# Eight relu(x - mean) tiles of layer 0 on VectorE instead of GpSimd, in a four-layer graph attention kernel

## The chip, the core and the metric

The kernel runs on one core of a Trainium2 chip. A core has five engines that work side by side, each with a queue of its own that is worked off in order: TensorE (PE in the profile, its weight loads PEld), VectorE (DVE), ScalarE (ACT), GpSimd (POOL) and SyncE (SP), which issues most of the transfers. Engines wait for each other through semaphores. The metric is the device time of one execution in microseconds; the time before is the median of three runs, 1781.22 us (1780.12 to 1788.01).

## The reference: what is computed

A graph of 4096 nodes with 256 features each goes through four layers of attention over one dense adjacency matrix of 4096 x 4096 integers, of which few entries are set. Every layer normalises the features, takes the positive part, and adds the layer's attention output to its input:

```python
h = jnp.maximum(_layernorm(x, axis=-1), 0.0)
x = x + _L0_gnn_ref(h, adj, ...)        # layers 1 to 3 likewise

# layer 0
h = node_features @ W.T + b_W
e = (h @ a1)[:, None] + (h @ a2)[None, :] + b_a[0]
e = jnp.where(e > 0, e, 0.2 * e)
scores = jnp.where(adjacency_matrix > 0, e, NEG_INF)
attention = jax.nn.softmax(scores, axis=1)
h_prime = attention @ h
```

Layer 1 has the same form with an ELU behind it, layer 2 has four heads of 64 features, layer 3 a positive and a negative softmax. The change touches only the first line of layer 0, for some of the nodes.

## The kernel before, in words

The 4096 nodes are 32 tiles of 128 nodes (NT = 32, P = 128); a block is 512 nodes, so four tiles (IB = 512, IT = 4). The node features x stay in SBUF as one tile of 128 x 32 x 256.

**Making the nodes of a layer.** `node_rows` (line 683) works on two tiles at a time. VectorE takes mean and variance (L693, L694); ScalarE makes 1/sqrt(variance + eps) through a logarithm and an exponential (L697, L698), which three small VectorE operations refine (L709 to L711). L702 makes z = max(x - mean, 0); the scale 1/std is positive and is applied only later. In layer 0 two GpSimd additions (L706) then add the layer's bias to x in place, since x is also the residual. TensorE transposes z in two halves (L716) into PSUM, ScalarE copies the result to SBUF as hT (L718), and `project` multiplies hT with the weights (L748) and lets ScalarE write the scaled rows g with their two exponentials (L759 to L783). z has four buffers (`bufs=4`), so z of a pair of tiles needs the buffers of the pair two before it, which are free once those have been transposed. The transposes, the projections and all small matmuls share two PSUM buffers (`s_mm`, `bufs=2`).

**Weights of layer 0.** `make_weights` (line 564) multiplies weights by attention vectors on TensorE (L622, L640); VectorE scales the results into columns of the weights (L634), sums a bias (L643, L644); TensorE spreads the bias row over all partitions (L647) and ScalarE copies it out (L649). L706 and the g of layer 0 need that copy.

**Attention of layer 0.** The first four blocks of target nodes (2048 targets) are treated as dense. For every block all 32 source tiles are gone through: VectorE makes the unnormalised weights s_p of 128 sources x 512 targets (L1033), and four times TensorE adds p.T @ g into an accumulator (L1071). On the way the adjacency is read in chunks of 1 MB, two transfers of 512 KB each (`s_raw`, L1306, four buffers). VectorE turns a chunk into a byte mask (L1325), which SyncE writes to DRAM for the later layers (L1327). The chunks of the other four blocks are read at the side, one every three steps, so that lists of the sources that matter to each tile can be built (lines 819 to 912: prefix sums, one-hot matrices L875, small matmuls L900, and the list itself L910). The last 16 tiles of targets, and most of the later layers, use such lists: GpSimd gathers the rows by indirect transfers (L929, L1231).

**What sets the order.** `run` (line 1194) goes through a plan of steps with leads of 0, 2, 3 and 6 steps for fetching, starting, weighing and multiplying, and takes a few pieces of work of other kinds after each step, `node_rows` among them, from queues. GpSimd's instructions stay in that program order (`tc.manual_schedule(engines={mybir.EngineType.Pool})`, line 1496). For the other four engines the framework that builds the program decides the order in each queue, from its own estimates of durations and from what each instruction depends on. When an instruction changes engine, the order of others in all these queues can change with it.

Of the kernel before, what the change touches and what calls it, by code (L numbers as in the profile page):

```python
# [13 lines left out]
ALU = mybir.AluOpType  # L14
# [9 lines left out]
IT = IB // P  # L24
# [455 lines left out]
def list_layers(ctx: ExitStack, tc: tile.TileContext, a: dict, out: bass.AP, flag):  # L480

    nc = tc.nc
# [31 lines left out]
    x = keep.tile([P, NT, D], F32, name="x")  # L514
# [17 lines left out]
    def feature_rows(l, jt):  # L532
        return table_rows(table[l], jt)[:, :, FRONT[l] : FRONT[l] + GW[l]]
# [13 lines left out]
    def weights(l, pool, prep, q):  # L547


        L = layers[l] = Layer()  # L550
        L.l = l
        L.H, L.part = LH[l], PART[l]

        ncols = D + 3 * L.H + (D if l == 3 else 0)
        L.w = pool.tile([P, 2, ncols], F32, name=f"s_w{l}", tag=f"s_w{l}")
        L.s = small.tile([P, NT, L.H], F32, name=f"s_s{l}", tag=f"s_s{l % 2}", bufs=1)
        L.ready = [False] * NT
        L.bias = None
        L.table = table[l]
        L.made = False  # L560
        L.making = make_weights(L, pool, prep, q)
        return L
# [120 lines left out]
    def node_rows(L, T0):  # L683


        u = f"{L.l}_{T0}"
        tiles = (T0, T0 + 1)
        while any(stored[T] < L.l - 1 for T in tiles) or not L.made:
            yield
        mv = small.tile([P, 2, 2], F32, name=f"s_mv_{u}", tag="mv")  # L690
        for k, T in enumerate(tiles):
            st6 = small.tile([P, 6], F32, name=f"s_st6_{u}_{k}", tag="st6")
            nc.vector.bn_stats(st6, x[:, T, :])  # L693
            nc.vector.bn_aggr(mv[:, k, :], st6)  # L694
            yield
        r = small.tile([P, 3, 2], F32, name=f"s_r_{u}", tag="r")
        nc.scalar.activation(r[:, 0], mv[:, :, 1], AF.Ln, bias=eps)  # L697
        nc.scalar.activation(r[:, 0], r[:, 0], AF.Exp, scale=-0.5)  # L698
        zs = []
        for k, T in enumerate(tiles):  # L700
            z = rows.tile([P, D], F32, name=f"s_z_{u}_{k}", tag="z", bufs=4)
            (nc.gpsimd if L.l == 0 else nc.vector).tensor_scalar(z, x[:, T, :], mv[:, k, 0:1], 0.0, op0=ALU.subtract, op1=ALU.max)  # L702
            zs.append(z)
        if L.bias is not None:
            for T in tiles:
                nc.gpsimd.tensor_add(x[:, T, :], x[:, T, :], L.bias[:, 0:D])  # L706
        yield 1.5

        nc.vector.scalar_tensor_tensor(r[:, 1], mv[:, :, 1], EPS, r[:, 0], op0=ALU.add, op1=ALU.mult)  # L709
        nc.vector.scalar_tensor_tensor(r[:, 1], r[:, 1], -0.5, r[:, 0], op0=ALU.mult, op1=ALU.mult)  # L710
        nc.vector.scalar_tensor_tensor(r[:, 2], r[:, 1], 1.5, r[:, 0], op0=ALU.add, op1=ALU.mult)  # L711
        hTs = []
        for k, T in enumerate(tiles):
            tp = ps_mm.tile([P, 2, P], F32, name=f"s_tp_{u}_{k}", tag="mm")
            for c in range(2):
                nc.tensor.transpose(tp[:, c, :], zs[k][:, c * P : (c + 1) * P], ident)  # L716
            hT = rows.tile([P, 2, P], F32, name=f"s_hT_{u}_{k}", tag="hT")
            nc.scalar.copy(hT, tp)  # L718
            hTs.append(hT)
            yield  # L720
        yield 1.5
        for k, T in enumerate(tiles):
            g = L.rows(T)
            yield from project(L, T, g, hTs[k], r[:, 2, k : k + 1])
            L.ready[T] = True
            if L.l == 0 and T % CH == CH - 1:
                nc.sync.dma_start(feature_rows(L.l, T), L.g[:, T - CH + 1 : T + 1, :])
            elif L.l > 0:
                nc.sync.dma_start(feature_rows(L.l, T)[:, T % CH, :], g)
# [251 lines left out]
    class Unit:  # L981
# [124 lines left out]
        def end(u):  # L1106
            l = u.L.l
            for it in range(u.nt):
                T = u.T0 + it
                if l == 0:  # L1110
                    end0(T, u.accs[it])
                else:
                    work = end2(u, it, T) if l == 2 else (end1 if l == 1 else end3)(T, u.accs[it])
                    push(posts, work, (4.0, 2.5, 0.0)[l - 1])
                if l < 3 and T % 2:
                    push(posts, node_rows(layers[l + 1], T - 1))
            if u.on_end:
                u.on_end()
# [129 lines left out]
    with ExitStack() as phase:  # L1248
# [8 lines left out]
        def load_x(b):  # L1257

            nc.sync.dma_start(
                x[:, b * IT : (b + 1) * IT, :],  # L1260
                a["x"][b * IB : (b + 1) * IB, :].rearrange("(c p) d -> p c d", p=P),
            )
            for T in (b * IT, b * IT + 2):
                push(posts, node_rows(L0, T))
# [135 lines left out]
    for l in (2, 3):  # L1400
        L = weights(l, late, late, nc.sync)
# [11 lines left out]
    for l in (1, 2, 3):  # L1413
        L = layers[l]
# [131 lines left out]
```

## Time and profile before

| what | us |
|---|---|
| median of three runs | 1781.22 |
| profiled execution | 1697.57 |
| its span | 1695.8 |
| TensorE busy in the span | 1619.6 (96%) |
| VectorE busy | 1321.9 (78%) |
| GpSimd busy | 959.8 (57%) |
| ScalarE busy | 632.6 (37%) |
| first attention matmul (L1071) starts | 30.48 |
| the 32 z of layer 0 on GpSimd | 9.96 to 92 |

The page counts one execution under the profiler. A group line names the source line, the engine, the operation, what is written and read, and how often; a duration follows. In a timeline the first number is the start in microseconds from the start of the span, the second the length, and a bracket tells how long the engine had been idle and what ended that. A line of the waits names who waited for whom, the sum, the number of times and the longest. A window's row gives the busy time of each engine in that stretch. Matmuls are pipelined and their ends are modelled, so a busy TensorE need not be one at its peak. The profiled execution is 84 us shorter than the median of the runs without a profile.

### The profile page before, as it was taken

The numbers are of one execution on the slowest core, as the hardware profiler recorded it, in microseconds if no ns is written. First come the engines' busy times: TensorE is split into PE (matmuls) and PEld (weight loads), VectorE is DVE, ScalarE is ACT, GpSimd is POOL, SyncE is SP. The second block draws the span as 40 slices with busy tenths as digits, with TensorE's granted clock in tenths as the row PEclk, the third lists the DMA queues.
The fourth block names the chain that finished last, engine by engine and source line by source line (L and its number), as shares of the span: only waits on it lengthen the run. The fifth ranks groups of instructions, "written<-read, shape, count | busy, mean of one in ns | idle before, by whom it ended". The sixth has DMA issues, their size and how long they took to land.

```text
span 1695.8 us, 29208 instructions
## 1 busy us (share of the span) xinstructions
PE 1619.6 (96%) x9268; PEld 1366.4 (81%) x9268; DVE 1321.9 (78%) x3908; ACT 632.6 (37%) x1915; POOL 959.8 (57%) x930
## 2 busy tenths in 40 slices
PE   6999999899989999879999999999999999999997
PEld 4887778788868887766787787899988888888886
DVE  6888999888845786558898988988884777777765
ACT  5631010120211232333667766899991111111111
POOL 9836766757635766651555444445652655555463
PEclk9999999999989999989999999999999999999998
DMA  8899879954364545452333333333434666666554
GB/s 270 281 326 291 277 231 273 309 155 124 76 170 129 151 131 165 138 149 67 92 97 96 89 86 99 86 100 95 132 106 125 204 187 180 178 184 173 171 169 118
DMA packets 152237, 274.70 MB, mean 162 GB/s; under 512 B 21423, under 2 KB 75340, under 8 KB 152076
## 3 DMA queue, kind: packets, MB, share of 16 engines
q0 software_dynamic: 45584, 130.39, 28.7%
q1 hardware_dynamic: 105656, 141.83, 26.0%
q8 instruction: 77, 1.26, 0.3%
q14 instruction: 84, 0.69, 0.1%
q10 hardware_dynamic: 836, 0.53, 0.1%
HBM read 231.76 MB, written 40.90 MB: 161 GB/s over the span
## 4 chain that ended last, share of the span: by engine, by line
PE 52%; DMA 2%; DVE 1%; ACT 1%; issue 0%; POOL 0%; ACTq 0%; DVEq 0%; POOLq 0%
PE s_acc L1071 24%; PE s_accm L1096 22%; PE s_pj L748 3%; DMA s_gg<-table,idx 2%; PE s_sT L967 1%; PE s_tp L716 1%; PE s_oT L1158 0%; ACT s_p L1019 0%; DVE s_p L1033 0%; ACT mlist L1056 0%; DMA out<-s_out 0%; DVE s_p L1042 0%; POOL s_gg L1231 0%; DVE s_y L1187 0%; DVE s_out L1138 0%
## 5 line engine op out<-in xcount | busy, mean ns | idle before, releaser
L1231 POOL DMA_INDIRECT s_gg<-table,idx x715 | 751.7, 1051 | 643.8 <-PE s_acc L1071 219.4
L1033 DVE SCALAR_TENSOR_TENSOR s_p<-s_grow,s_gg,mlist 128x128 f32<-128x128 f32 x994 | 316.3, 349 | 103.1 <-PE s_acc L1071 55.3
L1071 PE MATMUL s_acc<-s_gg,s_p 128*128 128x257 f32 x1430 | 348.1, 387 | 6.3 <-DVE s_p L1033 6.3
L1071 PEld LDWEIGHTS s_acc<-s_gg,s_p 128*128 128x128 f32 x1430 | 268.0, 192 | 47.9 <-DVE s_p L1033 11.5
L1071 PE MATMUL s_acc<-g,s_p 128*128 128x257 f32 x1152 | 283.4, 387 | 13.2 <-DVE s_p L1033 9.1
L1071 PEld LDWEIGHTS s_acc<-g,s_p 128*128 128x128 f32 x1152 | 214.0, 192 | 46.9 <-DVE s_p L1033 14.7
L1033 DVE SCALAR_TENSOR_TENSOR s_p<-s_grow,pre,mpre 128x128 f32<-128x128 f32 (+1 forms) x576 | 191.1, 371 | 39.3 <-PE s_acc L1071 31.9
L1096 PE MATMUL s_accm<-s_p,s_gg 128*65 128x128 f32 x1744 | 204.0, 273 | 0.0
L1071 PE MATMUL s_acc<-s_gs,s_p 128*128 128x257 f32 x896 | 203.7, 380 | 0.0
L1033 DVE SCALAR_TENSOR_TENSOR s_p<-s_grow,s_gs,s_ms 128x512 f32<-128x512 f32 x224 | 162.6, 752 | 48.0 <-PE s_acc L1071 23.1
L1096 PEld LDWEIGHTS s_accm<-s_p,s_gg 128*65 128x65 f32 x1744 | 193.1, 138 | 2.5
L1019 ACT ACTIVATE s_p<-s_grow,s_minus,s_gg 128x128 f32<-128x128 f32 x436 | 186.6, 486 | 13.4 <-PE s_accm L1096 7.9
L1071 PEld LDWEIGHTS s_acc<-s_gs,s_p 128*128 128x128 f32 x896 | 169.4, 190 | 25.1 <-DVE s_p L1033 1.1
L1071 PE MATMUL s_acc<-pre,s_p 128*128 128x257 f32 x768 | 181.6, 381 | 0.0
L973 ACT ACTIVATE s_grow<-s_sT 128x256 f32<-128x256 f32 (+2 forms) x136 | 46.7, 367 | 346.9 <-PE s_sT L967 310.8
L748 PE MATMUL s_pj<-s_w,s_hT 128*128 128x259 f32 (+3 forms) x640 | 165.3, 399 | 8.4 <-ACT s_hT L718 4.4
L1071 PEld LDWEIGHTS s_acc<-pre,s_p 128*128 128x128 f32 x768 | 143.5, 191 | 20.9 <-PE s_acc L1071 0.3
L929 POOL DMA_INDIRECT mlist<-mask_t,idx x105 | 123.9, 1180 | 61.8 <-issue 29.1
L748 PEld LDWEIGHTS s_pj<-s_w,s_hT 128*128 128x128 f32 x640 | 122.2, 198 | 33.7 <-ACT s_hT L718 8.4
L1096 PE MATMUL s_accm<-s_p,pre 128*65 128x128 f32 (+1 forms) x928 | 119.6, 284 | 0.0
L1096 PEld LDWEIGHTS s_accm<-s_p,pre 128*65 128x65 f32 x928 | 103.6, 138 | 16.6 <-issue 14.0
L1019 ACT ACTIVATE s_p<-s_grow,s_minus,pre 128x128 f32<-128x128 f32 x224 | 96.4, 487 | 19.1 <-issue 11.6
(126 smaller groups left out, 1741.0 us busy)
## 6 DMA issues: line engine op xcount, KB each, us to landing
s_raw<-in_adjT SPq DMA_DIRECT2D x128, 512.0 KB
s_gs<-table SPq DMA_DIRECT2D x28, 516.0 KB
s_gg<-table,idx POOLq DMA_INDIRECT x715, 3.6
mask_t<-s_m SPq DMA_DIRECT2D x35, 256.0 KB
table<-s_g SPq DMA_DIRECT2D x28, 258.0 KB
s_ms<-mask_t SPq DMA_DIRECT2D x28, 256.0 KB
table<-s_m SPq DMA_DIRECT2D x21, 256.0 KB
table<-g SPq DMA_DIRECT2D x8, 516.0 KB
```

Of the source, the lines that this page charges most:

```text
L716: nc.tensor.transpose(tp[:, c, :], zs[k][:, c * P : (c + 1) * P], ident)
L748: nc.tensor.matmul(ps, lhsT=hT[:, c, :], rhs=L.w[:, c, k * (D + 6) : k * (D + 6) + cols], start=(c == 0), stop=(c == 1),)
L929: nc.gpsimd.indirect_dma_start(out=mlist[:, OFFS[T] + k, :], out_offset=None, in_=mask_t[T // IT], in_offset=bass.IndirectOffsetOnAxis(ap= ...
L967: nc.tensor.transpose(ps[:, h - h0, it, :], L.s[:, T0 + it, h : h + 1].to_broadcast([P, P]), ident)
L973: nc.scalar.activation(grow[:, h1:h2, :], ps[:, h1 - h0 : h2 - h0].rearrange("p h a b -> p h (a b)"), AF.Exp, scale=scale,)
L1019: nc.scalar.activation(w[:, h, :], u.grow[:, h, :], AF.Relu, scale=g[h][:, n - 1 : n], bias=minus)
L1033: nc.vector.scalar_tensor_tensor(p[:, k, :], u.grow[:, h, :], g[k][:, n - 1 : n], m, op0=ALU.min if L.l == 3 and h == 1 else ALU.max, op1= ...
L1071: nc.tensor.matmul(u.accs[it][h], lhsT=p[:, k, it * P : (it + 1) * P], rhs=g[k][:, 0:n], start=first, stop=last,)
L1096: nc.tensor.matmul(u.regions[h], lhsT=g[k][:, 0 : DH + 1], rhs=p[:, k, :],  start=first and (u.nt > 1 or h == 0), stop=last, skip_group_ch ...
L1231: nc.gpsimd.indirect_dma_start(out=wide, out_offset=None, in_=L.table, in_offset=bass.IndirectOffsetOnAxis(ap=index[T][:, k : k + 1], axis=0),
```

## The change

In layer 0, L702 makes z on VectorE where the first of the two tiles is below tile 8 (T0 = 0, 2, 4, 6), so for tiles 0 to 7. Tiles 8 to 31 of layer 0 keep GpSimd, and layers 1 to 3 keep VectorE as before. The bias additions stay on GpSimd. Nothing else is written differently; the order in the queues of TensorE, VectorE, ScalarE and SyncE is decided anew when the program is built.

```diff
@@ def node_rows(L, T0):
         for k, T in enumerate(tiles):
             z = rows.tile([P, D], F32, name=f"s_z_{u}_{k}", tag="z", bufs=4)
-            (nc.gpsimd if L.l == 0 else nc.vector).tensor_scalar(z, x[:, T, :], mv[:, k, 0:1], 0.0, op0=ALU.subtract, op1=ALU.max)
+            (nc.gpsimd if L.l == 0 and T0 >= 2 * IT else nc.vector).tensor_scalar(z, x[:, T, :], mv[:, k, 0:1], 0.0, op0=ALU.subtract, op1=ALU.max)
             zs.append(z)
```

## The prediction, on record before the changed kernel ran

> **What bounds the kernel now.** I read the page's busy table and its slices first. TensorE is busy for 96% of the span, in nearly every slice but the first; that a busy TensorE is not one at its peak is allowed for below by looking at single stretches.
>
> ```profile
> span 1695.8 us, 29208 instructions
> PE 1619.6 (96%) x9268; PEld 1366.4 (81%) x9268; DVE 1321.9 (78%) x3908; ACT 632.6 (37%) x1915; POOL 959.8 (57%) x930
> PE   6999999899989999879999999999999999999997
> ```
>
> The changed instructions all lie in the first slice, so its windows come next, beside the windows in which the order of the work changes.
>
> ```profile
> 0.00:20.00 20.00, 8.09 (x26) 5.51 (x26) 10.47 (x48) 5.03 (x16) 18.14 (x54) 1.00 0.93 315
> 20.00:40.00 20.00, 17.12 (x75) 13.06 (x75) 15.37 (x39) 15.80 (x59) 18.70 (x17) 1.00 0.68 218
> 100.00:120.00 20.00, 20.00 (x119) 17.49 (x118) 17.59 (x32) 3.69 (x13) 1.44 (x1) 1.00 0.97 320
> 120.00:140.00 20.00, 17.91 (x122) 15.29 (x122) 17.52 (x44) 3.55 (x14) 14.71 (x13) 1.00 0.89 288
> 140.00:160.00 20.00, 19.54 (x106) 16.41 (x106) 15.28 (x33) 3.17 (x11) 12.78 (x12) 0.91 0.95 293
> 160.00:180.00 20.00, 15.77 (x82) 12.75 (x80) 18.57 (x48) 0.00 (x0) 16.04 (x14) 1.00 0.93 303
> ```
>
> Columns: window, length, busy time of PE, weight loads, DVE, ACT, POOL, then clock, DMA share, GB/s. GpSimd is busiest in the first two (18.14 and 18.70 of 20 us), which makes it look like the limit there. The timeline of the first 31 us and the waits of the first 60 us say what really ends last.
>
> ```profile
> 9.96 2.79 POOL L702 TENSOR_SCALAR s_z<-x,s_mv 128x256 f32<-128x256 f32 x2
> 11.65 0.14 DVE L643 TENSOR_TENSOR s_bias<-s_pb,s_ba 1x1 f32<-1x1 f32 x1
> 12.11 1.20 PE L647 MATMUL s_pbb<-s_bias,s_ones 1*128 1x258 f32 x2 [1.14 <-DVE s_r L709]
> 13.24 1.28 PE L716 MATMUL s_tp<-s_ident,s_z 128*128 128x128 f32 x4
> 15.48 0.29 ACT L697 ACTIVATE s_r<-s_mv,s_eps 128x2 f32<-128x2 f32 x1 [0.85 <-DVE s_mv L694]
> 15.92 0.63 ACT L718 COPY s_hT<-s_tp 128x256 f32<-128x256 f32 x2
> 20.44 0.47 ACT L783 ACTIVATE g<-s_pj,s_re 128x256 f32<-128x256 f32 x1
> 30.48 1.03 PE L1071 MATMUL s_acc<-g,s_p 128*128 128x257 f32 x4
> ```
>
> ```profile
> DVE s_mv L694 <- POOL s_z L702: 7.3, 4, 2.8
> PEld s_tp L716 <- POOL s_z L702: 3.1, 3, 1.6
> PE s_tp L716 <- POOL s_z L702: 0.9, 1, 0.9
> ```
>
> The first z is done at 9.96 + 2.79 = 12.75 us, but its transposes follow the bias matmul in TensorE's queue, which ends near 13.3. The hT copy then stands behind two pairs of rstd activations in ScalarE's queue, the second waiting for the mean of tiles 6 and 7. The transposes of tile 2 (21.0 us) are put down to z, but z_2 was done at 17.5; the PSUM buffer came free at 20.44 + 0.47 = 20.91, with ScalarE's g. So up to the first attention matmul at 30.48 the chain is TensorE and ScalarE in turn, with z on it at most at its head. From there to 118 us TensorE's timeline has no gap worth a number: a steady 5.73 us per four steps and two projected tiles.
>
> **What the Trainium skill says.** GPSIMD Engine Reference, section 4.1 Engine selection, calls one-input elementwise work on GpSimd roughly line-rate; here the measurement decides: the query of z gives a median of 1384 ns on GpSimd (32 times) and 347 ns on VectorE (12 times, layer 1), a factor of 4. Its section 8, Key points, says that GpSimd shares SBUF interfaces with VectorE, with contention; GpSimd's 1132 to 2297 ns for one form agrees, without proving it. TensorE: Matmul & The Clock Gate, Part 1, says that the array starts at half rate until it has been busy for a window of about 3.4 us; the trace agrees in kind: eight projection matmuls take 3.82 us at 16.32 and 2.02 us at 28.63.
>
> **The change part by part.** (1) Removed from GpSimd: four pairs of z, 2.79 + 2.25 + 2.69 + 2.25 = 9.98 us. Worth nothing by itself, since GpSimd's next work that anyone needs is z of tiles 8 and up, which waits for a buffer that a transpose of tile 4 frees (28.27 us), and the bias adds, read first at 119 us.
>
> (2) Added to VectorE: eight z at 0.33 us = 2.6 us. VectorE stood idle 8.13 to 10.84, 2.15 us at 21.58 and 2.85 us at 25.63, the last two for GpSimd's z, so idle time covers the sum; without that cover it would cost 2.6.
>
> (3) The start. In the built program VectorE's queue has z_0 right after its mean (about 6.6 us), then stands at L634 for the weights (10.84, as before), then the last mean of tiles 2 and 3, z_2 twice and one mask conversion, and only then the bias sum L643. Before, the conversion alone stood in between. The new work there: one aggregate 0.2 and two z at 0.27 start to start, 0.75 us. Bias sum 12.4, bias matmul 12.9, transposes 14.0, all 0.75 later. But ScalarE's queue now has hT directly behind the bias copy, and the rstd of tiles 4 to 7 after it. The bias copy ends near 14.4, the first transposed tile near 14.7: hT starts at 14.7 to 14.9 where it started at 15.92. That is 1.1 us early, and TensorE and ScalarE follow in the old order: first attention matmul at 29.4. The other end: if the clock window falls differently, the third and fourth projections (3.06 us, at 22.67) run at 2.0, a further gain of 1; or hT gains nothing and 0.75 is lost. So -2.1 to +0.75, and I take -1.1.
>
> (4) A new head-of-line wait: z_6 needs the buffer of z_2, freed by the transposes near 20 and 21 us. Queued behind it are mask conversions of the second chunk, the r of tiles 6 to 9, and the statistics of tiles 10 to 19. From z_6_1 (near 21.9) I count 4.6 us of VectorE work to the first s_p, so 26.5; the exponential it needs ends near 27. Covered, and the first matmul, behind the projection, leaves another 1.6.
>
> (5) Moved by the planner. On SyncE the first table write, which waits for g of tile 3 (near 26.5), stands in front of two 512 KB mask loads that had been issued by 23.2. So 1 MB starts late: at 350 GB/s 3 us of transfer. Its conversions come at about 33 on VectorE's new order, after landing, so no one waits. On VectorE conversions stand up to 2.8 us of work further back between 25 and 50 us, and 1.8 between 100 and 165, beyond the 2.6 of z; one-hot builds of the lists up to 4.7. TensorE's order changes from row 146 to 565, to about 165 us; behind that every queue is as before. TensorE full until 118, with 5 us of DMA room between 40 and 80 (share 0.82 to 0.90), hides the first; the second I put at 0, with as much as +-7: TensorE's idle in 120 to 180 is 2.1 + 0.5 + 4.2 = 6.8 us, so losing all of it gains 6.8 and doubling it loses 6.8.
>
> Sum: -1.1 against the profiled execution's 1697.57 us (span 1695.8). The median of the runs is 1781.22, 84 us longer; the profile doesn't show where, so I carry the difference over one to one: 1780.1.
>
> **The rivals.** A: GpSimd was the limit at the start. For it: 18.14 and 18.70 of 20 us, and 7.3 us of VectorE waits by name. Against: the ScalarE chain above. If all the 7.3 were on the path and the list stage gained too, 1781.2 - 7.3 - 3 = 1771. B, slower: the mask stream becomes late. Place: SyncE's queue from 23 us, where loads stand behind a write and behind late conversions. Price: 3 for the late megabyte, 2.8 and 1.8 for the conversions, 2.6 for z if nothing covers it: 10.2, so 1791.4. For it: DMA share 0.89 to 0.97 from 100 to 180, and TensorE's wait of 1.6 us at 139.74, behind a conversion that waited for its load. It decides once DMA's room between 40 and 80 is under about 5 us. C: nothing reaches the end, as the saved start is waited away at 138 for the same load: 1781.2. D: the list stage falls worse by a few waits of 2 us: 1785.
>
> **How the numbers follow.** Forecast 0.45, C 0.23, D 0.18, B 0.08, A 0.06. About 0.5% (8.9 us) is what a measurement can tell from no change here; the first three stay within it, with 0.02 of D beyond. Faster 0.06, same 0.84, slower 0.10. The range goes from just inside A's edge, 1773, to 1790: it leaves out most of A and B, and takes in the +-7 of step 5 and the spread of the runs (1780.12 to 1788.01).
>
> **What would show it.** z on VectorE at 0.33 to 0.45 us, the first near 6.7; the bias matmul near 12.9 instead of 12.11; hT near 14.8; the first attention matmul at 29.4 (28.4 to 31.2); TensorE without gaps from there to 118; the first two table-blocked loads issued after 26 us. I am wrong if the first attention matmul comes before 27 (A), or if TensorE waits for s_p between 30 and 118, or for more than 10 us between 118 and 180 (B, D). Behind 180 us the stretches should keep their lengths; if they don't, the cause lies outside these steps.

## The result: no difference in two comparisons, 0.1% faster in the most exact one

| comparison with the kernel before, on the same chip | before, us | changed, us | ratio, 95% interval |
|---|---|---|---|
| first result | 1783.49 (20 runs) | 1784.40 (20 runs) | 1.0007 [0.9984, 1.0030] |
| repeat, group 1 | 1788.41 (59) | 1787.02 (22) | 1.0001 [0.9981, 1.0021] |
| repeat, group 3 | 1701.01 (37) | 1698.69 (22) | 0.9988 [0.9978, 0.9998] |

I predicted 1780.1 us with a range of 1773 to 1790 and "same" at 0.84. The first measurement is 1784.4, inside the range, and its difference from before is inside 0.5%. The last row has the narrowest interval: 0.0012 x 1701 = 2.0 us faster, with an interval of 0.3 to 3.7 us. That isn't proof of a gain: the other two rows include no change, and the unchanged kernel against itself gave 1.0028 and 0.9997 in groups 1 and 3. Absolute times are to be compared only within a row, since the unchanged kernel took 1788, 1798 and 1701 us on the chips of the three groups of runs below, and three traces of executions between 1780 and 1787 us show 23 to 32 us of TensorE idle time under "issue" (a wait for nothing that the profile shows) where the profile before and those of group 3 show 0.4 us or less.

So the profile of the changed kernel that came with the first result (span 1786.5 us) can't be subtracted from that of before (1695.8) as a whole. Its page:

```profile
span 1786.5 us, 29188 instructions
PE 1661.1 (93%) x9268; PEld 1387.1 (78%) x9268; DVE 1321.3 (74%) x3916; ACT 633.1 (35%) x1915; POOL 951.5 (53%) x922
PE   7998899799989899888999999988989999999997
```

The eight z show in the counts: VectorE 3908 to 3916, GpSimd 930 to 922. GpSimd is busy 8.3 us less, and TensorE is still the busiest. The start of the execution, up to the first attention matmul, can be compared. Windows of the changed kernel (window, length, busy time of PE, weight loads, DVE, ACT, POOL, then clock, DMA share, GB/s):

```profile
0.00:20.00 20.00, 8.00 (x30) 5.62 (x30) 13.00 (x49) 6.50 (x22) 13.31 (x52) 1.00 0.93 315
20.00:40.00 20.00, 18.63 (x90) 14.54 (x89) 18.68 (x54) 16.40 (x63) 16.50 (x15) 1.00 0.72 238
```

GpSimd goes from 18.14 to 13.31 us in the first window, VectorE from 10.47 to 13.00, and TensorE gains 1.5 us in the second (17.12 to 18.63). The timeline of the changed kernel (start, length, what, and in brackets the idle time before it and its end) can be read beside that of before:

```profile
6.56 2.54 DVE L702 TENSOR_SCALAR s_z<-x,s_mv 128x256 f32<-128x256 f32 x2
12.25 0.14 DVE L643 TENSOR_TENSOR s_bias<-s_pb,s_ba 1x1 f32<-1x1 f32 x1
12.72 1.19 PE L647 MATMUL s_pbb<-s_bias,s_ones 1*128 1x258 f32 x2 [1.74 <-DVE s_bias L644]
13.84 1.22 PE L716 MATMUL s_tp<-s_ident,s_z 128*128 128x128 f32 x4
14.57 0.37 ACT L718 COPY s_hT<-s_tp 128x256 f32<-128x256 f32 x1 [0.24 <-PE s_tp L716]
14.99 3.06 PE L748 MATMUL s_pj<-s_w,s_hT 128*128 128x259 f32 x8
20.17 2.02 PE L748 MATMUL s_pj<-s_w,s_hT 128*128 128x259 f32 x8
26.97 1.03 PE L1071 MATMUL s_acc<-g,s_p 128*128 128x257 f32 x4
```

The bias sum is 0.6 us later than before (11.65), as the two z of tiles 2 and 3 now stand ahead of it. In spite of that hT starts 1.35 us earlier (15.92 before), because it stands directly behind the bias copy in ScalarE's queue. The next two groups of eight projections take 3.06 and 2.02 us, where before took 3.82 and 3.06. The first attention matmul comes at 26.97 instead of 30.48.

The clock column reads 1.00 in these first windows, but it counts the time ahead of the trace's first clock record as full clock. That record, of full clock, comes at 24.98 us before and at 17.15 us here, and a projection matmul takes 640 ns ahead of it and 380 ns behind it in both. The first two groups of projections are 0.76 and 1.04 us shorter for it, so up to 1.8 us of the 3.5 are due to where the clock became full. And the waits of the first 60 us of the changed kernel:

```profile
DVE s_mv L694 <- POOL s_z L702: 2.6, 3, 1.3
PEld s_tp L716 <- POOL s_z L702: 0.3, 1, 0.3
```

The waits with GpSimd's z as the one named have shrunk from 7.3 to 2.6 us and from 3.1 to 0.3.

### The profile page after: what moved, and what is told of

Same layout as the page of the kernel before. It is cut to its first block, busy times and chain, and to the rows that moved or that the text cites. A ratio compares the mean times of both kernels' runs of the same rounds, so it can differ in the third digit from the quotient of the medians.

```text
span 1786.5 us, 29188 instructions
## 1 busy us (share of the span) xinstructions
PE 1661.1 (93%) x9268; PEld 1387.1 (78%) x9268; DVE 1321.3 (74%) x3916; ACT 633.1 (35%) x1915; POOL 951.5 (53%) x922
## 3 DMA queue, kind: packets, MB, share of 16 engines
q8 instruction: 77, 1.26, 0.3%
## 4 chain that ended last, share of the span: by engine, by line
PE 77%; DVE 8%; issue 4%; DMA 4%; ACT 3%; another core or an unknown queue 2%; POOL 1%; SPq 0%; DVEq 0%; ACTq 0%; POOLq 0%
PE s_acc L1071 45%; PE s_accm L1096 19%; PE s_pj L748 7%; DVE s_p L1033 3%; DMA s_gg<-table,idx 2%; PE idx_ps L900 2%; PE s_sT L967 2%; PE s_tp L716 1%; ACT s_p L1019 1%; DVE s_m L1325 1%; DMA s_raw<-in_adjT 1%; POOL s_gg L1231 1%; DVE first L875 1%; DVE s_p L1042 1%
## 5 line engine op out<-in xcount | busy, mean ns | idle before, releaser
L1033 DVE SCALAR_TENSOR_TENSOR s_p<-s_grow,s_gg,mlist 128x128 f32<-128x128 f32 x994 | 309.0, 344 | 143.1 <-PE s_acc L1071 73.3
L1071 PE MATMUL s_acc<-s_gg,s_p 128*128 128x257 f32 x1430 | 354.3, 390 | 8.4 <-DVE s_p L1033 5.2
L1071 PE MATMUL s_acc<-g,s_p 128*128 128x257 f32 x1152 | 299.6, 402 | 17.7 <-DVE s_p L1033 7.9
L1071 PEld LDWEIGHTS s_acc<-s_gg,s_p 128*128 128x128 f32 x1430 | 270.0, 194 | 53.3 <-DVE s_p L1033 11.1
L1071 PEld LDWEIGHTS s_acc<-g,s_p 128*128 128x128 f32 x1152 | 222.9, 201 | 55.6 <-DVE s_p L1033 11.6
L1096 PE MATMUL s_accm<-s_p,s_gg 128*65 128x128 f32 x1744 | 208.4, 275 | 1.2 <-issue 1.0
L1071 PE MATMUL s_acc<-s_gs,s_p 128*128 128x257 f32 x896 | 203.7, 380 | 0.0
L1096 PEld LDWEIGHTS s_accm<-s_p,s_gg 128*65 128x65 f32 x1744 | 196.9, 140 | 4.7 <-issue 2.2
L1071 PEld LDWEIGHTS s_acc<-s_gs,s_p 128*128 128x128 f32 x896 | 169.5, 190 | 25.1 <-DVE s_p L1033 1.1
L1071 PE MATMUL s_acc<-pre,s_p 128*128 128x257 f32 x768 | 184.3, 385 | 3.9 <-issue 2.9
L973 ACT ACTIVATE s_grow<-s_sT 128x256 f32<-128x256 f32 (+2 forms) x136 | 46.7, 367 | 374.4 <-PE s_sT L967 246.5
L1071 PEld LDWEIGHTS s_acc<-pre,s_p 128*128 128x128 f32 x768 | 144.7, 193 | 26.5 <-issue 4.2
```

The lines of the kernel that those rows point to most:

```text
L973: nc.scalar.activation(grow[:, h1:h2, :], ps[:, h1 - h0 : h2 - h0].rearrange("p h a b -> p h (a b)"), AF.Exp, scale=scale,)
L1033: nc.vector.scalar_tensor_tensor(p[:, k, :], u.grow[:, h, :], g[k][:, n - 1 : n], m, op0=ALU.min if L.l == 3 and h == 1 else ALU.max, op1= ...
L1071: nc.tensor.matmul(u.accs[it][h], lhsT=p[:, k, it * P : (it + 1) * P], rhs=g[k][:, 0:n], start=first, stop=last,)
L1096: nc.tensor.matmul(u.regions[h], lhsT=g[k][:, 0 : DH + 1], rhs=p[:, k, :],  start=first and (u.nt > 1 or h == 0), stop=last, skip_group_ch ...
```

## The experiments

I kept three questions apart: where the early start comes from, whether it reaches the end, and what the list stage does with it. Theory T1: the new order of the queues, hT ahead of later rstd work above all, makes the start early, and TensorE's clock adds to it. Rival T2: it comes from z being made sooner by a faster engine, or from GpSimd being relieved (rival A of the prediction).

### The two kernels again

No edit; the kernel before and the changed one once more, on one chip.

> The kernel before, unchanged, timed against itself and profiled once more. The profiled execution of the kernel before was 84 us shorter than its runs. If that was one unusual execution, this profile is 1770 to 1805 us long like the runs, the ratio is 1.000 within 0.004, and the first attention matmul starts again at 30.5 us (29.5 to 31.5), since the start has no dependence on what differed. If the profile as such shortens the kernel, it is near 1697 again. If the start varies from execution to execution as the whole does, the first attention matmul is off by 2 us or more, and the 3.5 us by which it came earlier in the changed kernel (26.97) mean little.

> The changed kernel once more. Theory (the start is 3.5 us earlier and the end gains about as much): ratio 0.998, too near to 1 for these rounds (their interval is about 0.004 to each side); first attention matmul at 27.0 (26.5 to 27.5). Rival (the new order of the list stage gives it back or more): ratio 1.000 to 1.004 with the same early start.

The unchanged kernel against itself gave 1.0028 [0.9996, 1.0059], the change 1.0001 [0.9981, 1.0021]. So some 0.3% can't be told from nothing in this group. The traces are sharper. Timeline of the unchanged kernel:

```profile
16.30 0.63 ACT L718 COPY s_hT<-s_tp 128x256 f32<-128x256 f32 x2
16.70 3.82 PE L748 MATMUL s_pj<-s_w,s_hT 128*128 128x259 f32 x8 [1.80 <-ACT s_hT L718]
32.77 1.03 PE L1071 MATMUL s_acc<-g,s_p 128*128 128x257 f32 x4
```

and of the changed one:

```profile
14.65 0.37 ACT L718 COPY s_hT<-s_tp 128x256 f32<-128x256 f32 x1 [0.24 <-PE s_tp L716]
15.07 3.82 PE L748 MATMUL s_pj<-s_w,s_hT 128*128 128x259 f32 x8
29.48 1.03 PE L1071 MATMUL s_acc<-g,s_p 128*128 128x257 f32 x4
```

Again 3.3 us between them. Both are about 2.4 us later than in the first pair of profiles (30.48 and 26.97): the third group of projections fell into a half-clock piece (granted clock 0.55 and 0.54 around it) and took 3.69 and 3.70 us. Where these pieces fall differs from execution to execution.

### Does a shifted start reach the end?

```diff
-            nc.scalar.copy(L.bias[:, 0 : D + 2], pb)
+            for _ in range(100): nc.scalar.copy(L.bias[:, 0 : D + 2], pb)
```

> The kernel before with the copy of the bias row on ScalarE made 100 times instead of once, which puts some 26 to 31 us (0.26 to 0.31 us each, the distance of the two hT copies) in front of the first scaled rows g and so of the first attention matmul. It measures what a microsecond of the start is worth at the end. Theory (TensorE is the limit behind the start, so the start counts one to one): the end is later by as much as the first attention matmul, 1.015 to 1.018. Rival (TensorE waits for the mask stream further on, so that a later start is in part absorbed): at most two thirds of it, 1.010 or less.

The first attention matmul came at 69.85 us, 37.1 later than in the unchanged kernel of that group; the whole took 1.0168 [1.0132, 1.0205] of it, 0.0168 x 1788.41 = 30.0 us more (23.6 to 36.7). So 0.64 to 0.99 of a shift reaches the end. My numbers assumed a delay of 26 to 31 us and were too small, since the copies took 0.41 us each; that the ratio lies inside the range I gave for it is luck. Most of a shift is carried through. That all of it is (what I had put into the forecast) is just outside the interval, and since the start of one kernel moves by 2 us from trace to trace, it isn't excluded. The delay also changed the order of other queues, and from the first attention matmul to the growb before the list stage (L973, 163.87) it is 94.0 us here where the unchanged kernel has 87.1, so this is not a pure shift.

### The order alone: a miss, and why

z stays on GpSimd; the index fills of the lists (L790 to L815) are called behind the first pair of z instead of at the start, so that these z can be early on GpSimd too. With that the order in TensorE's, ScalarE's and SyncE's queues becomes that of the changed kernel.

```diff
-        consts = list_constants(lists_p)
+        consts = []; hooks[0] = lambda: consts.extend(list_constants(lists_p))
...
-        if L.bias is not None:
+        if (L.l == 0 and hooks.pop(T0, int)() and 0) or L.bias is not None:
```

> The kernel before with z on GpSimd for all tiles, but with GpSimd's long index fills (7 us, from 2.97 to 9.98) put behind the first pair of z instead of ahead of it. So z of tiles 0 and 1 is there near 9.5 instead of 12.75 while the work of VectorE stays as it was. In the program as built the queues of TensorE, ScalarE and SyncE then have exactly the order of the changed kernel. Theory (the earlier start comes from the order, hT ahead of the rstd of tiles 4 to 7, and not from VectorE's speed): hT at 14 to 15, first attention matmul at 26 to 28. Since VectorE has no z in front of the bias sum, hT may even be 0.5 us earlier than in the changed kernel; against that, z of tiles 2 and 3 comes behind the fills, near 18.5 to 20.5, against a need at 18.9. Rival (VectorE's faster z is what counts): hT as before at 15.9, first attention matmul at 30 to 31. Ratio 0.998, or 1.000 to 1.003 if the new order of the list stage costs.

hT came only at 16.42, no earlier than in the unchanged kernel of the group (16.30). The first attention matmul came at 32.09 against 32.77, but the third group of projections took 2.02 us here and 3.69 there; beside a trace of the unchanged kernel with the same three groups (3.82, 3.01 and 2.02 us, first matmul at 30.54, the last section of the experiments) it is 1.55 us late. Ratio 1.0030 [1.0009, 1.0051]. Its timeline tells why:

```profile
9.04 4.61 POOL L790 IOTA place<- 128x1792 f16 x1
11.14 3.04 DVE L1325 TENSOR_SCALAR mpre<-s_raw 128x1024 uint8<-128x1024 int32 x1
14.11 0.13 DVE L643 TENSOR_TENSOR s_bias<-s_pb,s_ba 1x1 f32<-1x1 f32 x1
15.80 0.38 ACT L649 COPY s_bias_all<-s_pbb 128x258 f32<-128x258 f32 x1 [8.04 <-PE s_pbb L647]
16.42 0.37 ACT L718 COPY s_hT<-s_tp 128x256 f32<-128x256 f32 x1 [0.24 <-PE s_tp L716]
32.09 1.14 PE L1071 MATMUL s_acc<-g,s_p 128*128 128x257 f32 x4 [0.98 <-DVE s_p L1033]
```

hT does stand right behind the bias copy, 0.62 us after it, where the unchanged kernel of the group had 2.58 (13.72 to 16.30). But the moved fill now ran beside the second mask conversion, which took 3.04 us instead of 0.94, and the bias sum behind it was 2.1 us late. The order gained 2 us at hT and the collision took them. The last line shows one more wait, 0.98 us for VectorE's s_p; the next experiment tells where that comes from.

### The order alone, without the collision

The same edit with the fills behind the z of tiles 24 and 25 (`hooks[24]`), near 73 us, in two forms: with z on GpSimd as before, and in the changed kernel.

> z stays on GpSimd; the index fills (L790 to L815, 7 us of GpSimd) move from the start to behind the z of tiles 24 and 25, where they collide with nothing at the start. The order of TensorE's, ScalarE's and SyncE's queues is that of the change. T1 (the order makes the gain; the run with the fills just behind the first z missed it because the fill then ran beside the second mask conversion, L1325, and made it 3.04 us instead of 0.94, so that the bias sum L643 came at 14.11 instead of 12.03): second L1325 at 0.8 to 1.4 us, L643 at 11.5 to 12.6, first s_hT copy at 14.3 to 15.3, first L1071 at 27 to 30.5 although GpSimd makes every z. T2 (VectorE's faster z makes it): s_hT copy after 16, first L1071 after 31.5. Whole time: 0.997 to 1.004 of before; the 7 us of fills may hold up z of tiles 26 to 31 by up to 5 us, seen as TensorE idle between 70 and 100.

Timeline, with every z on GpSimd:

```profile
11.04 0.68 DVE L1325 TENSOR_SCALAR mpre<-s_raw 128x1024 uint8<-128x1024 int32 x1
11.64 0.14 DVE L643 TENSOR_TENSOR s_bias<-s_pb,s_ba 1x1 f32<-1x1 f32 x1
13.96 0.37 ACT L718 COPY s_hT<-s_tp 128x256 f32<-128x256 f32 x1 [0.24 <-PE s_tp L716]
29.64 1.14 PE L1071 MATMUL s_acc<-g,s_p 128*128 128x257 f32 x4 [2.66 <-DVE s_p L1033]
```

hT starts 0.7 us earlier than in the repeat of the change, although GpSimd makes every z, so T1 holds for hT. The first attention matmul, at 29.64, lies in T1's range too, but it waited 2.66 us for VectorE's s_p, which the changed kernel doesn't show. VectorE's timeline ahead of that s_p says why:

```profile
21.15 0.18 DVE L694 BATCH_NORM_AGGREGATE s_mv<-s_st 128x2 f32<-128x6 f32 x1 [2.73 <-POOL s_z L702]
25.21 0.18 DVE L694 BATCH_NORM_AGGREGATE s_mv<-s_st 128x2 f32<-128x6 f32 x1 [1.74 <-POOL s_z L702]
28.86 0.73 DVE L1033 SCALAR_TENSOR_TENSOR s_p<-s_grow,g,mpre 128x512 f32<-128x512 f32 x1
```

The means wait for GpSimd's z, which still reads those of earlier tiles, and s_p stands behind them. With the second and third groups of projections at full clock (2.02 us each here), the changed kernel with all z of the start on VectorE reached its first matmul at 27.5 to 27.8 (in the runs of 32 tiles and of group 3 below). So T1 is half of the truth: the order brings hT forward by itself, and some 2 us of what it could bring reach the first matmul only if GpSimd's z don't hold VectorE up, which is T2's share. Whole time 1.0034 [1.0007, 1.0062].

The old order has the same second limit close to its first. In a run of the kernel before whose queues keep the old order up to the first attention matmul (idx_first_before, below) the second and third groups happened to fall into full clock:

```profile
22.31 2.02 PE L748 MATMUL s_pj<-s_w,s_hT 128*128 128x259 f32 x8
26.02 0.25 DVE L694 BATCH_NORM_AGGREGATE s_mv<-s_st 128x2 f32<-128x6 f32 x2 [2.85 <-POOL s_z L702]
30.54 1.13 PE L1071 MATMUL s_acc<-g,s_p 128*128 128x257 f32 x4 [1.26 <-DVE s_p L1033]
```

The first matmul came no earlier than in the profile before (30.48), where the second group took 3.06 us and s_p was ready at 30.05: what the clock gave was waited away for s_p, behind means that had waited for GpSimd's z. Its partner with the change (idx_first_after, second and third groups of 2.02 us too) has its first matmul at 27.53. Of these 3.0 us at like clock, 1.7 are hT's (16.30 against 14.62) and 1.3 are the wait that is gone.

> The change, with the index fills behind the z of tiles 24 and 25; every queue but GpSimd's has the order of the change. If the fill is what made VectorE's first z 1.17 and 1.44 us long, both take 0.31 to 0.40 us now and the mask conversion beside them 0.8 us. If the length has another cause (first use of the data, waiting for the write of x), they stay above 1 us. First L1071 27 to 30.5 us, as z is not on the path at the start. Whole time 0.995 to 1.004 of before, with the fills again able to cost up to 5 us between 70 and 100.

The first two z of the changed kernel, with no fill beside them:

```profile
6.59 0.58 DVE L702 TENSOR_SCALAR s_z<-x,s_mv 128x256 f32<-128x256 f32 x2
```

0.58 us for the pair where the changed kernel took 2.54, so the fill was what made them long. hT did not move (14.69), so these z are not on the path to it. The clock became full late in this trace (second group of projections 3.06 us, third 2.02), and the first attention matmul came at 29.18. Beside the unchanged kernel with nearly the same three groups (30.54) that is 1.36 us early, and hT is 1.33 early (16.02 there): with the clock late in both, the gain is hT's alone. Whole time 1.0013 [0.9985, 1.0041].

### Two tiles, and all 32

```diff
-            (nc.gpsimd if L.l == 0 and T0 >= 2 * IT else nc.vector).tensor_scalar(z, ...)
+            (nc.gpsimd if L.l == 0 and T0 >= 2 else nc.vector).tensor_scalar(z, ...)
```

> VectorE makes z of tiles 0 and 1 alone; the order of TensorE's, ScalarE's and SyncE's queues is that of the change. Theory T1 (the start gain comes from the new order, which the first pair of z alone brings about): first copy of s_hT (L718) at 14.4 to 15.2 us and first attention matmul (L1071) at 27 to 30.5, as in the two traces of the change (26.97, 29.48). Rival T2 (it comes from all eight z being ready sooner): half of it or less, first L1071 at 31 us or later. The z of tile 0 and 1 take 1.1 to 1.5 us each where GpSimd's index fill runs beside them.

Timeline with z of tiles 0 and 1 alone on VectorE:

```profile
14.66 0.37 ACT L718 COPY s_hT<-s_tp 128x256 f32<-128x256 f32 x1 [0.24 <-PE s_tp L716]
29.91 1.13 PE L1071 MATMUL s_acc<-g,s_p 128*128 128x257 f32 x4 [0.24 <-DVE s_p L1033]
```

The same hT, and a first matmul 0.4 us behind that of the repeat of the change (29.48): two of the eight z are enough for the order. That z of tiles 2 to 7 on GpSimd cost nothing here proves little, since a third group of projections at half clock (3.70 us) covers what they might have cost. This kernel had one execution, so its time says nothing.

For all 32 tiles the line reads `nc.vector.tensor_scalar(z, ...)`.

> VectorE makes z of all 32 tiles of layer 0: four times the dose, with the same order of TensorE's, ScalarE's and SyncE's queues. T1 (z on GpSimd is covered, the start alone counts): the same start as the change (first L1071 27 to 30.5 us), TensorE gapless from there to about 118 us, ratio to before 0.996 to 1.001. Rival A (GpSimd's z held the dense stage up): first ScalarE growb (L973, last before the list stage) 3 us or more closer to the first L1071 than the 87.1 to 87.6 us seen so far, ratio below 0.995. Rival V (VectorE becomes the limit of the dense stage: 57 us busy in the 70 us from 30 to 100, plus 24 z of 0.33 to 1.4 us): that distance grows beyond 89 us, ratio above 1.002.

Window 30 to 100 us, all 32 on VectorE:

```profile
30.00:100.00 70.00, 69.94 (x344) 58.93 (x344) 61.74 (x158) 45.55 (x166) 20.91 (x24) 1.00 0.91 303
```

The same window of the repeat of the change:

```profile
30.00:100.00 70.00, 69.86 (x345) 58.68 (x344) 54.84 (x128) 46.27 (x171) 55.27 (x47) 1.00 0.88 299
```

GpSimd falls from 55.27 to 20.91 us, VectorE rises from 54.84 to 61.74, and TensorE is as full as before. From the first attention matmul (27.55) to the growb before the list stage (L973, 115.17) it is 87.62 us, as in the repeat of the change (117.09 - 29.48 = 87.61). Rival A falls for the dense stage: 34 us less of GpSimd's work bought nothing there. VectorE doesn't become the limit either (rival V, a distance beyond 89 us). The ratio, 1.0038 [1.0011, 1.0065], missed T1's range by 0.003 and lies where V had put it; an unchanged kernel had read 1.0028 in group 1, so I don't take it for a loss, though group 2 has no repeat of the unchanged kernel that would show it. (All traces with the new order have 87.5 to 88.0 us here, those with the old order 87.0 to 87.1, but for slow_bias and one with late loads: half a microsecond of the start goes in the dense stage.)

### Where the start's gain goes: the list index, a theory that fell

In the changed kernel VectorE converts the first list index (L910) 4.95 us behind L973, in the kernel before 0.51 us behind it: the normalising of the next layer has slipped in front. GpSimd's first 22 gathers wait for that index; in the traces of group 1 they start at 122.48 with the change and at 120.83 without, although TensorE is 2.8 us ahead by then. I took this for the place where the gain is lost, and preferred the conversion:

```diff
-            nc.vector.tensor_scalar(idx, ps[:, 0:cap], float(HALF), None, op0=ALU.add)
+            with tc.high_priority(): nc.vector.tensor_scalar(idx, ps[:, 0:cap], float(HALF), None, op0=ALU.add)
```

> The change, with the framework told to prefer the list's index conversion (L910). In the built program the first L910 stands right behind the first s_p of the second dense block, no longer behind 5 us of normalising and statistics. Theory L (the gain at the start is lost because the new order converts the first list index 4.4 us later, so GpSimd's 22 gathers start no earlier): first L910 within 1 us of the growb L973 before the list stage (0.5 in the kernel before, 4.95 in the change), first gather L929 at 116 to 119 us (120.83 in the repeat of before, 122.48 in the repeat of the change), end of the 22 gathers at 148 to 151.5 (153.9 and 153.4), next gather at 159 to 163 (164.73 and 164.64), ratio to before 0.995 to 1.000. Rival S (TensorE's slow stretch near 150 to 160 us sets the next gather whatever comes before): first gather early as above, but the next gather behind the 22 still at 163 to 166 and the ratio 0.999 to 1.003.

> The kernel before with the same preference for L910. There the conversion came 0.5 us behind L973 already, so theory L expects next to nothing: first L910 0 to 0.6 us from L973, start as in the kernel before (first L1071 30.5 to 33), ratio 0.997 to 1.003. If the preference helps in other ways (the later lists), the ratio is below 0.997 here too, and then a gain of the other kernel isn't L's.

The first gather came at 115.47, even earlier than expected, and the 22 ended at 147.6; but the next gather came at 156.55, hardly before the 157.82 of the changed kernel on that chip. The waits from 115 to 160 us say what it waited for; with the preference:

```profile
POOL s_gg L1231 <- PE s_acc L1071: 8.9, 1, 8.9
PEld s_acc L1071 <- DVE s_p L1033: 4.7, 3, 2.0
```

and in the changed kernel of the same group:

```profile
POOL s_gg L1231 <- PE s_acc L1071: 4.6, 1, 4.6
PEld s_acc L1071 <- DVE s_p L1033: 1.5, 1, 1.5
```

What GpSimd gained at the front it waited away at the end, for buffers that TensorE's attention matmuls free. The whole became slower, 1.0045 [1.0026, 1.0065], and on the kernel before 1.0075 [1.0049, 1.0102], where the index had not been late at all. So theory L falls: TensorE, not the index, sets that point, and the changed kernel's own 4.6 us of waiting said so already. The test isn't a pure one, since the preference also made TensorE wait 3.2 us longer for s_p. What the preference costs lies behind it: hT copies that are 0.6 us apart from those of the changed kernel at 258 us are 7.1 us apart at 306 (313.55 against 306.43). Which of the later lists does that I didn't try.

### Both kernels once more, on a quieter chip

No edit.

> The kernel before, unchanged: a third trace of the old order and a second look at what the comparison gives without a change. First L1071 30.5 to 33 us, first L910 0.5 us after L973, first gather 118 to 121.5, next gather behind the 22 at 157 to 166, ratio 0.997 to 1.003 (1.0028 the first time).

> The change, unchanged: a third trace and a third measurement of the whole. First L1071 26.5 to 30, first L910 4.9 to 5.1 us after L973, first gather 119.9 to 123, ratio 0.998 to 1.003 (1.0007 and 1.0001 so far).

Unchanged 0.9997 [0.9984, 1.0009], change 0.9988 [0.9978, 0.9998]: the interval excludes no change by little. The profile of the changed kernel here can at last be laid beside the first profile of the kernel before (span 1695.8 us), as its page shows:

```profile
span 1697.3 us, 29188 instructions
PE 1621.7 (96%) x9268; PEld 1367.3 (81%) x9268; DVE 1326.3 (78%) x3916; ACT 632.7 (37%) x1915; POOL 951.9 (56%) x922
```

| event | before (first profile), us | changed, us | difference |
|---|---|---|---|
| first hT copy (L718) | 15.92 | 14.67 | -1.25 |
| first attention matmul (L1071) | 30.48 | 27.82 | -2.66 |
| growb before the list stage (L973) | 117.60 | 115.44 | -2.16 |
| third hT copy of the list stage (L718) | 141.26 | 138.42 | -2.84 |
| next hT copy | 204.96 | 204.12 | -0.84 |
| hT copy near 259 | 259.26 | 258.10 | -1.16 |
| ScalarE's L1134, first | 525.85 | 524.39 | -1.46 |
| ScalarE's L1134, 17th | 643.26 | 642.03 | -1.23 |
| ScalarE's L1134, 25th | 742.61 | 743.05 | +0.44 |
| end (span) | 1695.8 | 1697.3 | +1.5 |

Of the 2.66 us at the first matmul, 1.25 are hT's and 1.04 the third and fourth projections' (3.06 us before, 2.02 now). Up to 141 us the gain is whole but for the half microsecond of the dense stage, which comes back there; between 141 and 205 about 2 us of it go. Windows of the changed kernel there:

```profile
148.00:154.00 6.00, 6.00 (x25) 4.87 (x24) 5.06 (x11) 0.00 (x0) 3.97 (x5) 0.65 1.04 310
141.00:205.00 64.00, 59.80 (x351) 49.59 (x350) 55.75 (x126) 3.76 (x14) 47.48 (x41) 0.92 0.90 282
```

and of the kernel before:

```profile
148.00:154.00 6.00, 6.00 (x49) 5.42 (x48) 4.02 (x9) 0.99 (x4) 4.01 (x5) 1.00 0.95 279
141.00:205.00 64.00, 58.29 (x359) 48.82 (x358) 56.97 (x128) 3.98 (x15) 48.09 (x41) 0.97 0.88 281
```

The granted clock is 0.65 from 148 to 154 and 1.00 before: 0.35 x 6 = 2.1 us of full clock missing. Over the whole stretch it is 0.92 against 0.97, 0.05 x 64 = 3.2 us, while TensorE is idle for 1.5 us less (4.2 against 5.7): a loss of 1.7 us, about what the table shows. So waits are not what took the gain. Whether the new order brings the half-clock piece there or it fell there by chance one trace each doesn't tell; this stays open. Behind about 180 us the queues have the order of before (the prediction had 165). The step from -1.23 to +0.44 is again one of the clock: between these two rows the changed kernel's trace has one half-clock piece of 3.4 us more (at 678 us), worth 1.7 us. I take it, and the way on to +1.5, for a difference between two executions; that is argued from the order, not shown.

The other trace of this group, of the unchanged kernel, has a span of 1703.1 us, so against it the change ends 5.8 us early where the table has +1.5: two traces can't tell what the whole gains. It is no help for the middle either: mask conversions waited for their loads between 72 and 95 us (the longest 2.99 us), TensorE then waited 2.98 us at 96, and L973 came at 122.48, 91.9 us after the first attention matmul (30.54) instead of 87.1.

## Why the prediction was right, by its own steps

**(1) GpSimd relieved, worth nothing: right for the dense stage, not for the start.** All 32 z on VectorE took 34 us from GpSimd's window and left the dense stage at 87.6 us. But my reading that z stands on the chain "at most at its head" looked at the one chain that ended last, and another ended 0.4 us ahead of it: GpSimd's z hold VectorE's means, and so s_p. In the old order at full clock the first matmul waited 1.26 us for s_p, and in the new order with z on GpSimd 2.66 us. That the change takes z away too is why the gain lasts to the first matmul.

**(2) 2.6 us on VectorE, covered: the cover right, the size wrong.** My sign of 0.33 to 0.45 us for a z failed for four of the eight. They took 2.44 + 0.58 + 1.47 + 0.35 + 0.34 = 5.2 us in the last trace, not 2.6: two beside the index fill 1.2 us each, two beside GpSimd's bias adds 0.7. I had taken the duration of layer 1's z, which have no such neighbour. The idle time of VectorE held the double too.

**(3) The start: direction and mechanism right, size too small.** The bias sum came at 12.25 to 12.36 (12.4 forecast), the bias matmul at 12.72 to 12.82 (12.9), hT at 14.57 to 14.67 (14.7 to 14.9). The term that I mis-sized is the way from there to the first matmul: I took -1.1 for the whole, and it was -2.7 to -3.5, as hT gained 1.25 to 1.65 and the third and fourth projections ran at full clock. That was the "other end" of the step (-2.1), and it happened in all three traces of the changed kernel. In part it is luck: the clock became full near 25 us in all three traces of the kernel before, but at 19.7 in idx_first_before, and at 23.6 in the changed kernel with the fills moved. Whether the new order makes an early full clock more likely is open. And the "other end" left something out: with z on GpSimd the faster projections would have been waited away for s_p.

My own sign, "wrong if the first attention matmul comes before 27 (A)", was touched by the first profile, with 26.97. It was a bad sign: a clock piece that falls well brings the same number, and A, in which GpSimd's load would have been worth 7.3 us, isn't what happened: only the 1.3 to 2.7 us of step 1 are of its kind.

**(4) z of tile 6 in VectorE's queue: covered, right.** Its halves started at 19.4 to 20.2 and at 21.0 to 21.8 us (near 20 and 21.9 forecast), and no s_p was late for them.

**(5) The planner's moves: hidden in the dense stage, right; 0 in the list stage, as good as could be told.** The two loads behind the table write went out at 24.6 (25.5 in the last trace), not after 26, since g was early too. TensorE was busy for 87.87 of the 88 us from 30 to 118. From 118 to 180 it was idle for 5.7 us in the last trace (8.5 in the first result's, with its "issue" waits), against 6.8 before, so neither rival B nor D showed. Rival C may have in part: in the one pair of traces that can be compared, about 2 us of the start went between 141 and 205, though for TensorE's clock and not, as C has it, for a late load at 138.

**The sum.** -1.1 forecast, -2.0 (-3.7 to -0.3) measured where it could be measured best. The start brought 1.6 us or more beyond what I had said; how much of that the list stage kept is known from one pair of traces only. That all of it was within a measurement's error of 0.5% is why "same" was safe: a forecast of no change at all would have come as near, so the whole time confirms none of the steps, and only the traces do. The 4 us between 1780.1 and 1784.4 are what runs differ by: the kernel before, timed again, went from 1781.22 to 1783.49.

## What to carry to other kernels

An engine that is busy for 90% of a window and named in most waits need not be its limit: follow the chain to the first instruction that someone waits for, and see what stands in front of it in its own queue. But ask too which other chain ends near it, and how near: here it ended 0.4 us ahead of the matmul (s_p at 30.05, the matmul at 30.48), and became the limit as soon as the first got faster. Where a program decides the order of the queues, an instruction's new engine and the new order it brings have to be costed together, since each decides what the other is worth; so build the changed kernel and read the queues around the chain first. A duration from another stage is only good if the neighbour on the other engine is the same: here an elementwise operation took up to 4.5 times as long (1.44 against 0.32 us).

## What the runs showed of the hardware

- **VectorE beside GpSimd.** One z (128x256 f32) on VectorE takes 0.32 to 0.35 us; beside GpSimd's index fills 1.17 and 1.44, beside its additions 0.73 and 0.81, and with the fills moved away the first pair took 0.58 together. One mask conversion (128x1024, int32 to uint8) took 0.68 us with no fill beside it and 3.04 beside the large fill. The statistics (L693) stayed at 0.39 to 0.41 us beside the same fills. What can be seen is where the slow ones end: the two z at 7.73 and 9.10 us, 0.14 and 0.15 behind the ends of the fills beside them (7.59 and 8.95), and the conversion at 14.18, 0.53 behind the fill's end (13.65), as if they waited for GpSimd's instruction to end. What makes one operation suffer and another not is not shown.
- **Where the half-clock pieces fall moves the start by as much as the change does.** In the changed kernel the first eight projections took 3.06 or 3.82 us and the third eight 2.02 or 3.70, and the first attention matmul of the changed kernel came at 26.97, 29.48 and 27.82 in three traces.
